# Expert tiles of 128 places at the end of an expert's list, in the expert layer of a conv-attention hybrid

## The chip, the cores and the metric

The kernel runs on one core of a Trainium2 chip, in one launch. The metric is the device time in microseconds; the time of a kernel is the median of its runs.

## What is computed

The reference is four layers over 4 images of 1,024 tokens with 256 channels, all float32: a Mamba-like layer with a squeeze gate, a non-local block, attention followed by a mixture of experts (layer 2), and an efficient attention followed by an LSTM (layer 3). The change lies in the mixture of experts:

```python
B, L, D, H, E = (8, 4096, 256, 1024, 8)         # sizes of H and E are used; D is 256
xf = x.reshape(-1, D)                           # 4096 tokens, normalised
gate_logits = xf @ Wg + bg
top_w, top_i = jax.lax.top_k(gate_logits, 2)
top_w = jax.nn.softmax(top_w, axis=-1)
w_dense = jnp.sum(jax.nn.one_hot(top_i, E) * top_w[..., None], axis=1)
out = 0
for e in range(E):
    h = jax.nn.gelu(xf @ W1[e] + b1[e], approximate=False)
    out = out + w_dense[:, e:e + 1] * (h @ W2[e] + b2[e])
```

Every token picks two of eight experts, so there are 8,192 picks. The input is fixed by a seed, and so is how many picks each expert gets.

## The kernel before

The kernel does not compute all eight experts for all tokens. It sorts the picks into lists, one for each expert, and cuts every list into tiles of `TW` = 256 places, each of `SUB` = 2 groups of 128 places (one place for each partition). The last tile of a list is padded with places that point to spare rows.

**Two lots.** The first lot, `early`, has `EARLY` = 16 tiles made from the first three images, and it is planned while the attention of the fourth image still runs (`_plan_early`, L906). The second lot, `late`, has the rest. Only a number of late tiles that always suffices can be unrolled without a test; `TILES` = 23 is the most that can come about, `FIRM` = 20 are run always, and the three beyond lie behind a branch. The branch tests `v.used`, the number of late tiles that the lists need, which each engine reads into a register (L830, L831).

**The plan.** `_plan_late` (L941) works on VectorE: it takes the number of picks of each expert from a small matmul, counts the tiles in it by comparing with 0, 256, 512 and so on (L947, L948), subtracts those taken early, and sums up to the end and the begin of each expert's tiles. `_tile_weights` (L878) turns this into the row of the expert's weights for every tile. `_of_picks` (L892) looks up one number for each pick, such as where its expert begins. `_table` (L1003) compares the place of each pick with all places (L1016), and 64 small bf16 matmuls into `p_t` (L1024) turn that into the list of rows to gather, `rows`, and a mark for first or second choice, `second`. The table of the late lot is made beside the first early tiles.

**One tile.** `_expert_tiles` (L1119) runs the tiles of a list in order. For each one:

- Weights: one indirect DMA on GpSimd's queue (L1091) gathers the whole expert, 128 rows of 4,360 float32 numbers, into one of three buffers. It is issued two tiles ahead.
- Rows: two indirect DMAs (L1101), one for each group of 128 places, issued three tiles ahead.
- `turn`: four transposes (L1128) into `p_x` and one copy to `xT` on VectorE (L1132), one tile ahead.
- First product: for each of 8 parts of the hidden layer, two matmuls with 256 columns (L1152) into `ph`, which has two buffers, and a Gelu with bias on ScalarE (L1155) into `hT`.
- Second product: for each group of 128 places, eight matmuls with 256 columns (L1162) into `po`, which has two buffers; then bias and gate on VectorE (L1173, L1174) and a scatter-add into `acc` in DRAM (L1175, GpSimd's queue).

When all tiles are done, `acc` is read back into `rows` for layer 3 (L1732).

**Order of the work.** The experts' stage is ordered by a planner that places the instructions of each engine by its own estimate of costs; within an engine the order is then fixed. The layers' LSTM at the end is ordered by hand. A float32 matmul leaves two records in the trace, a transpose one.

Of the kernel before, what the change touches and what calls it, by code (L numbers as in the profile page):

```python
# [9 lines left out]
F32 = mybir.dt.float32  # L10
# [8 lines left out]
P = 128  # L19
# [24 lines left out]
SUB = TW // P  # L44
NE = NT - TPI
EARLY = (2 * NE * P - E * (TW - 1)) // TW
TILES = (2 * T + E * (TW - 1)) // TW - EARLY
FIRM = 2 * T // TW + E // 2 - EARLY
G = 16
AWAY = 1024.0  # L50
NMOE = C * HID + NHC * D + NHC + D
# [751 lines left out]
        s.last.append(lambda: _plan_late(s, single))  # L803


def _layer2_experts(s, beside):

    nc, tc, v = s.nc, s.tc, s.plan
    with ExitStack() as ctx:
        pool = ctx.enter_context(tc.tile_pool(name="moe", bufs=2))
        ps = ctx.enter_context(tc.tile_pool(name="moe_ps", bufs=2, space=PSUM))
        s.fetch.pools.append(pool)

        def aside(k):  # L820
            if k == 0:
                p = ps.tile([P, 2, TILES * SUB], F32, name="p_t", bufs=1)
                _table(s, pool, p, v.late)
            if k == EARLY // 2:
                beside()

        for f in s.last:
            f()
        _expert_tiles(s, pool, ps, s.tiles, aside)
        used = nc.values_load(v.used[0:1, 0:1], min_val=0, max_val=TILES)  # L830
        with tc.If(used > FIRM):  # L831
            tiles = [(v.late, i) for i in range(FIRM, TILES)]
            _fetch_first(s, tiles)
            _expert_tiles(s, pool, ps, tiles)
    s.choice.close()
# [39 lines left out]
        s.nc.vector.tensor_add(v.before[:, n, :], v.before[:, n - 1, :], both[:, n - 1 - first, :])  # L875


def _tile_weights(s, tab):  # L878

    nc, v = s.nc, s.plan  # L880
    n = tab.tiles
    past = v.past[:, :n, :]
    nc.vector.tensor_tensor(past, _bc(tab.end, 1, n), _bc(v.by_tile[:, :n], 2, E), ALU.is_le)
# [3 lines left out]
    nc.vector.scalar_tensor_tensor(  # L887
        tab.weights, expert, float(P), v.slot.to_broadcast([P, n]), ALU.mult, ALU.add
    )


# [14 lines left out]
def _plan_early(s, pool, slim):  # L906


    nc, v = s.nc, s.plan
    tab = v.early  # L910
    count = slim()[:, :E]
    nc.tensor.matmul(count, s.ones, v.before[:, NE, :], start=True, stop=True)

    nc.vector.scalar_tensor_tensor(
        v.over, _bc(count, 2, T // TW), 0.5 - TW, _bc(v.edge, 1, E), ALU.add, ALU.is_gt
    )
    full = v.full
    nc.vector.tensor_reduce(full, v.over, AX.X, ALU.add)
    nc.vector.tensor_tensor_scan(tab.end, s.ones[:, :E], full, 0.0, ALU.mult, ALU.add)
    nc.vector.tensor_sub(tab.begin, tab.end, full)  # L920
    nc.vector.tensor_scalar(v.taken, tab.begin, -1.0, float(EARLY), ALU.mult, ALU.add)
    nc.vector.tensor_scalar_max(v.taken, v.taken, 0.0)
    nc.vector.tensor_tensor(v.taken, v.taken, full, ALU.min)
    _tile_weights(s, tab)
    stop = pool.tile([P, E], F32, name="stop")
    nc.vector.tensor_add(stop, tab.begin, v.taken)
    for x in (tab.begin, stop):
        nc.vector.tensor_scalar_mul(x, x, float(SUB))
    half = v.half[:, :NE].rearrange("p n i -> p (n i)")
    tab.place = _of_picks(s, pool, "which", tab.begin, NE)  # L930
    nc.vector.tensor_add(tab.place, tab.place, half)
    done = _of_picks(s, pool, "stops", stop, NE)
    nc.vector.tensor_tensor(done, tab.place, done, ALU.is_lt)
    nc.vector.scalar_tensor_tensor(half, done, AWAY, half, ALU.mult, ALU.add)
    nc.vector.tensor_scalar(done, done, -AWAY, AWAY, ALU.mult, ALU.add)
    nc.vector.tensor_add(tab.place, tab.place, done)
    p = slim()[:, : 2 * EARLY * SUB].rearrange("p (v h) -> p v h", v=2)
    _table(s, pool, p, tab)


def _plan_late(s, slim):  # L941

    nc, v = s.nc, s.plan
    tab = v.late
    count = slim()[:, :E]
    nc.tensor.matmul(count, s.ones, v.before[:, NT, :], start=True, stop=True)
    nc.vector.tensor_tensor(v.over, _bc(count, 2, T // TW), _bc(v.edge, 1, E), ALU.is_gt)  # L947
    nc.vector.tensor_reduce(v.full, v.over, AX.X, ALU.add)  # L948
    nc.vector.tensor_sub(v.full, v.full, v.taken)
    nc.vector.tensor_tensor_scan(tab.end, s.ones[:, :E], v.full, 0.0, ALU.mult, ALU.add)  # L950
    nc.vector.tensor_sub(tab.begin, tab.end, v.full)
    nc.vector.tensor_sub(tab.begin, tab.begin, v.taken)
    nc.vector.tensor_scalar_mul(tab.begin, tab.begin, float(SUB))
    _tile_weights(s, tab)
    nc.vector.tensor_copy(v.used, tab.end[:, E - 1 :])
    tab.place = None


# [44 lines left out]
def _table(s, pool, p_t, tab):  # L1003
# [1 line left out]


    nc, v = s.nc, s.plan
    n, h = tab.tokens, tab.tiles * SUB
    place = tab.place
    if place is None:  # L1010
        place = _of_picks(s, pool, "place", tab.begin, n)
        nc.vector.tensor_add(place, place, v.half[:, :n].rearrange("p n i -> p (n i)"))
    for g in range(2 * n // G):
        at = bass.ts(g, G)
        own = pool.tile([P, G, h], BF16, name="own")
# [27 lines left out]
def _plan_constants(s, pool):  # L1043
    nc = s.nc
    v = s.plan = SimpleNamespace()
    v.picks = pool.tile([P, NT, 2, E], BF16, name="picks")
    v.half = pool.tile([P, NT, 2], F32, name="half")
    v.left = pool.tile([P, NT, 2, P], BF16, name="left")
    v.before = pool.tile([P, NT + 1, E], F32, name="before")
    n = max(EARLY, TILES)  # L1050
    for name, shape in (
        ("over", [E, T // TW]), ("full", [E]), ("taken", [E]), ("past", [n, E]), ("expert", [n]),
    ):
        setattr(v, name, pool.tile([P, *shape], F32, name=name))
    v.used = pool.tile([P, 1], I32, name="used")
    for name, tokens, tiles in (("early", NE, EARLY), ("late", NT, TILES)):
        tab = SimpleNamespace(tokens=tokens, tiles=tiles, xn=s.xn if tokens == NT else s.xn_early)
        for key, shape, dtype in (
            ("end", [E], F32), ("begin", [E], F32), ("weights", [tiles], I32),
            ("rows", [tiles * SUB], I32), ("second", [tiles * SUB, 2], F32),  # L1060
        ):
# [4 lines left out]
    v.halves = _iota(s, pool, "halves", n * SUB, 1)  # L1066
# [12 lines left out]
def _fetch(s, pool):  # L1079
# [16 lines left out]

    def rows(tab, i):
        got = []
        for j in range(SUB):
            r = pool.tile([P, D + 2], F32, name=f"r{j}", bufs=4)  # L1100
            nc.gpsimd.indirect_dma_start(  # L1101
                out=r, out_offset=None, in_=tab.xn, in_offset=at(tab.rows, i * SUB + j)
            )
            got.append(r)
        f.got.append(got)

    f.weights, f.rows, f.at = weights, rows, at


def _fetch_first(s, tiles):  # L1110
# [8 lines left out]
def _expert_tiles(s, pool, ps, tiles, aside=None):  # L1119
# [2 lines left out]
    nc, tc, f = s.nc, s.tc, s.fetch  # L1122

    def turn(rows):
        p_x = ps.tile([P, C, TW], F32, name="p_x", bufs=1)
        for j in range(SUB):
            for k in range(C):
                nc.tensor.transpose(  # L1128
                    p_x[:, k, bass.ts(j, P)], rows[j][:, bass.ts(k, P)], s.ident
                )  # L1130
        xT = pool.tile([P, C, TW], F32, name="xT")
        nc.vector.tensor_copy(xT, p_x)  # L1132
        return xT

    xT = turn(f.got[0])
    for i, (tab, number) in enumerate(tiles):
# [8 lines left out]
            f.rows(*tiles[i + 3])  # L1145
        if i + 2 < len(tiles):
            f.weights(*tiles[i + 2])
        hT = pool.tile([P, NHC, TW], F32, name="hT")
        for m in range(NHC):
            ph = ps.tile([P, TW], F32, name="ph")  # L1150
            for k in range(C):
                nc.tensor.matmul(  # L1152
                    ph, w1[:, k, bass.ts(m, P)], xT[:, k, :], start=k == 0, stop=k == C - 1
# [1 line left out]
            nc.scalar.activation(hT[:, m, :], ph, AF.Gelu, bias=b1[:, m : m + 1])  # L1155
        if i + 1 < len(tiles):
            xT = turn(f.got[0])
        for j in range(SUB):
            n = number * SUB + j
            po = ps.tile([P, D], F32, name="po")  # L1160
            for m in range(NHC):
                nc.tensor.matmul(  # L1162
# [546 lines left out]
def conv_attn_hybrid_kernel(ctx: ExitStack, tc: tile.TileContext, d: dict, out: bass.AP):  # L1709
# [121 lines left out]
```

## Time and profile before

| | |
|---|---|
| median of 3 runs | 3441.82 us (3440.3 to 3443.47) |
| the profiled execution's own time | 3442.45 us |
| its span, from first to last instruction | 3440.7 us |
| mean granted TensorE clock | 0.985 |
| TensorE busy, share of the span | 3119.8 us, 91% |
| VectorE, ScalarE, GpSimd busy | 1837.7, 1097.0, 533.3 us |
| first and last matmul of L1152 | 710.5 us and 1226.4 us |
| last scatter-add issued, `acc` read back | 1235.8 us, 1241.9 us |

The experts' stage is thus some 525 us of 3,441. In the lines of the profile, L12 is line 12 of the kernel before. A group's row has the line, the engine, the operation, what it writes and reads with shapes, and its number; then the busy time in us and the mean duration of one in ns; then the idle time of the engine before it and what ended most of that. PE is TensorE's matmul, PEld its weight load (shown apart, since it overlaps), DVE is VectorE, ACT ScalarE, POOL GpSimd, SP SyncE. In order of time, a row has the start and the duration in us, and in brackets the idle time ahead and what ended it. A busy TensorE is not TensorE at its peak, because the ends of matmuls are modelled and overlap; the spacing from start to start says what one costs in a row of them.

### The profile page before, as it was taken

The numbers are of one execution on the slowest core, as the hardware profiler recorded it, in microseconds if no ns is written. First come the engines' busy times: TensorE is split into PE (matmuls) and PEld (weight loads), VectorE is DVE, ScalarE is ACT, GpSimd is POOL, SyncE is SP. The second block draws the span as 40 slices with busy tenths as digits, with TensorE's granted clock in tenths as the row PEclk, the third lists the DMA queues.
The fourth block names the chain that finished last, engine by engine and source line by source line (L and its number), as shares of the span: only waits on it lengthen the run. The fifth ranks groups of instructions, "written<-read, shape, count | busy, mean of one in ns | idle before, by whom it ended". The sixth has DMA issues, their size and how long they took to land.

```text
span 3440.7 us, 143780 instructions
## 1 busy us (share of the span) xinstructions
PE 3119.8 (91%) x63650; PEld 2505.1 (73%) x63650; DVE 1837.7 (53%) x8205; ACT 1097.0 (32%) x4339; POOL 533.3 (16%) x749
## 2 busy tenths in 40 slices
PE   8797899999999989998998998998998998998887
PEld 5476577678888856777777777777777777777776
DVE  5785644651111143565555565655655665555555
ACT  5763222222222222332332332332332332332222
POOL 2252100124444320001001001001001001001000
PEclk9898999999999989999999999999999999999999
DMA  2000011356666620000000000000000000000000
GB/s 82 1 1 2 9 37 38 107 168 197 193 193 193 189 62 1 4 4 9 5 4 8 6 4 9 6 4 8 6 4 8 6 4 8 6 4 8 7 4 10
DMA packets 49459, 138.94 MB, mean 40 GB/s; under 512 B 4992, under 2 KB 38336, under 8 KB 44224
## 3 DMA queue, kind: packets, MB, share of 16 engines
q0 software_dynamic: 19008, 99.32, 9.4%
q1 hardware_dynamic: 27680, 24.45, 2.2%
q8 instruction: 499, 8.18, 1.0%
q10 hardware_dynamic: 2144, 5.95, 0.5%
q14 instruction: 128, 1.05, 0.1%
HBM read 104.21 MB, written 25.49 MB: 38 GB/s over the span
## 4 chain that ended last, share of the span: by engine, by line
PE 28%; DVE 20%; ACT 10%; issue 5%; DMA 1%; ACTq 0%; POOL 0%; DVEq 0%; SPq 0%
PE pre L1657 16%; DVE col L1668 11%; PE pre L1600 6%; ACT tri L1671 5%; DVE scan L1680 5%; DVE hs L1691 4%; PE p_a L1554 3%; PE p_d L1258 1%; PE p_k L1226 1%; DMA acc<-y,late_rows 1%; ACTq L1671 0%; PE p_w L165 0%; PE p_d L1266 0%; PE p_w L1246 0%; PE p_u L1388 0%
## 5 line engine op out<-in xcount | busy, mean ns | idle before, releaser
L1657 PE MATMUL pre<-w_v,hs 128*4 128x64 f32 x49104 | 872.9, 219 | 210.2 <-DVE hs L1691 199.2
L1657 PEld LDWEIGHTS pre<-w_v,hs 128*4 128x4 f32 x49104 | 684.1, 86 | 398.8 <-DVE hs L1691 397.1
L1600 PE MATMUL pre<-xg,pick 128*128 128x64 f32 x6144 | 903.9, 283 | 0.5 <-DVE xg L1567 0.5
L1600 PEld LDWEIGHTS pre<-xg,pick 128*128 128x128 f32 x6144 | 763.5, 191 | 118.4 <-DVE xg L1567 1.2
L1668 DVE STREAM_TRANSPOSE col<-pre 128x64 f32<-128x64 f32 x2048 | 485.2, 250 | 304.5 <-PE pre L1657 289.2
L1671 ACT ACTIVATE tri<-col 128x16 f32<-128x16 f32 x1024 | 229.4, 224 | 1178.6 <-DVE col L1668 1178.6
L1680 DVE TENSOR_TENSOR_SCAN scan<-tri 128x24 f32<-128x24 f32 x1024 | 216.3, 211 | 361.8 <-ACT tri L1671 361.8
L1562 POOL TENSOR_TENSOR xg<-xg,gate_bias 128x192 f32<-128x192 f32 x127 | 74.8, 589 | 1605.6 <-ACT xg L1561 1605.6
L1152 PE MATMUL ph<-xT,wt 128*128 128x256 f32 x1152 | 256.3, 380 | 1.6 <-issue 0.9
L1162 PE MATMUL po<-wt,hT 128*128 128x256 f32 x1152 | 255.7, 379 | 0.0
L1155 ACT ACTIVATE hT<-ph,wt 128x256 f32<-128x256 f32 x288 | 136.1, 473 | 360.2 <-PE ph L1152 354.3
L1152 PEld LDWEIGHTS ph<-xT,wt 128*128 128x128 f32 x1152 | 207.1, 189 | 43.2 <-ACT hT L1155 6.1
L1162 PEld LDWEIGHTS po<-wt,hT 128*128 128x128 f32 x1152 | 216.0, 190 | 27.8
L1689 DVE STREAM_TRANSPOSE gate<-row 128x64 f32<-128x64 f32 x1024 | 228.3, 223 | 0.7
L1678 ACT ACTIVATE row<-pre 128x64 f32<-128x64 f32 x1024 | 210.3, 205 | 0.6
L1696 DVE SCALAR_TENSOR_TENSOR tri<-hs,scan 128x8 f32<-128x8 f32 x1023 | 182.1, 178 | 36.2 <-DVE hs L1691 1.7
L1132 DVE COPY xT<-p_x 128x512 f32<-128x512 f32 x36 | 24.9, 691 | 211.2 <-PE p_x L1128 211.0
L1173 DVE TENSOR_TENSOR y<-po,wt 128x256 f32<-128x256 f32 x72 | 30.6, 424 | 193.9 <-PE po L1162 184.3
L1554 PE MATMUL p_a<-w_u,u 128*32 128x192 f32 x1792 | 119.3, 338 | 0.0
L732 PE MATMUL p_s<-u,q 128*128 128x512 f32 x256 | 117.0, 597 | 0.0
L766 PE MATMUL p_w<-v,prT 128*128 128x256 f32 x512 | 116.0, 379 | 0.7 <-ACT prT L758 0.7
L766 PEld LDWEIGHTS p_w<-v,prT 128*128 128x128 f32 x512 | 95.5, 190 | 15.5 <-issue 2.9
(2441 smaller groups left out, 3287.6 us busy)
## 6 DMA issues: line engine op xcount, KB each, us to landing
xn<-xn SPq DMA_DIRECT2D x8, 516.0 KB, 3.6
x<-in_x_dram SPq DMA_DIRECT2D x16, 256.0 KB, 2.9
acc<-rows SPq DMA_DIRECT2D x8, 512.0 KB, 2.9
out_dram<-part SPq DMA_DIRECT2D x64, 64.0 KB, 1.7
xn_early<-xn SPq DMA_DIRECT2D x6, 516.0 KB, 4.9
rows<-acc SPq DMA_DIRECT2D x6, 512.0 KB, 8.1
w_l<-in_w_l_dram ACTq DMA_DIRECT2D x1, 1092.0 KB, 10.2
rows<-acc SPq DMA_DIRECT2D x4, 256.0 KB, 4.2
```

The lines of the kernel that those rows point to most:

```text
L766: nc.tensor.matmul(p, prT[:, n, :], images[g // TPI].v[:, n, :], start=n == 0, stop=n == TPI - 1)
L1152: nc.tensor.matmul(ph, w1[:, k, bass.ts(m, P)], xT[:, k, :], start=k == 0, stop=k == C - 1)
L1162: nc.tensor.matmul(po, hT[:, m, bass.ts(j, P)], w2[:, m, :], start=m == 0, stop=m == NHC - 1)
L1554: nc.tensor.matmul(p[32 * j : 32 * (j + 1), :], u3[i * SG // P][:, k, bass.ts(i % (P // SG), 32)], w_u[:, k, j * Q : (j + 1) * Q], start=k ...
L1600: nc.tensor.matmul(p, pick[:, r].rearrange("p j r -> p (j r)"), xg[i][:, v], start=True, stop=t == 0,)
L1657: nc.tensor.matmul(p[32 * j : 32 * j + B, :], hs[:, t - 1, k * B : (k + 1) * B], w_v[:, k, j * Q + v.start : j * Q + v.stop], start=False, ...
L1668: nc.vector.transpose(col[:, g * C : (g + 1) * C, :].rearrange("p n r -> p (n r)"), pre[t % 2][g])
L1671: nc.scalar.activation(z[:, 2:50].rearrange("p (g q) -> p g q", g=2)[:, :, ::3].rearrange("p g (k b) -> p (g k) b", k=C), col[:, :, :B], A ...
L1678: nc.scalar.activation(row, pre[t % 2][2], AF.Tanh)
L1680: nc.vector.tensor_tensor_scan(scan, z[:, 0 : 3 * S], z[:, 26 : 26 + 3 * S], 0.0, ALU.mult, ALU.add)
L1689: nc.vector.transpose(gate.rearrange("p n r -> p (n r)"), row)
L1696: nc.vector.scalar_tensor_tensor(tri[(t + 1) % 2][:, 28:52:3], h, 0.5, cell, ALU.mult, ALU.mult)
```

## The change

A list may now end in a half tile. If the rest of an expert's picks over full tiles is 1 to 128, that rest goes into a tile of one group of 128 places; a rest of 129 to 255 still makes a full tile. The second lot consists of `TILES` = 19 full tiles and `HALVES` = 8 half tiles at most. Of these 17 full and 4 half tiles are always run; the half ones lie after the 4th, 8th, 12th and 16th full tile of the late lot, and the last tile is a full one. The 2 full and 4 half tiles beyond lie behind the branch, which now tests whether more than 17 full or more than 4 half tiles are needed. A half tile gathers the expert's whole weights and one group of rows, transposes two blocks, runs its first product with 128 columns and its second product for one group. The plan counts full tiles and half tiles apart and gives the picks of an odd end their own places, behind all full ones. The early lot is not changed.

```diff
-TILES = (2 * T + E * (TW - 1)) // TW - EARLY
-FIRM = 2 * T // TW + E // 2 - EARLY
+TILES = (2 * T + E * (P - 1)) // TW - EARLY
+HALVES = E
+FIRM = 2 * T // TW + 1 - EARLY
+FIRM_HALVES = E // 2
...
+def _late(tab, first, last, first_half, last_half):
+
+    tiles = [(tab, i) for i in range(first, last)]
+    n = last_half - first_half
+    step = max(len(tiles) // n, 1)
+    for i in reversed(range(n)):
+        tiles.insert(step * (i + 1), (tab, TILES + first_half + i))
+    return tiles
...
-                p = ps.tile([P, 2, TILES * SUB], F32, name="p_t", bufs=1)
+                p = ps.tile([P, 2, v.late.places], F32, name="p_t", bufs=1)
...
-        used = nc.values_load(v.used[0:1, 0:1], min_val=0, max_val=TILES)
-        with tc.If(used > FIRM):
-            tiles = [(v.late, i) for i in range(FIRM, TILES)]
+        rest = nc.values_load(v.rest[0:1, 0:1], min_val=0, max_val=TILES)
+        with tc.If(rest > 0):
+            tiles = _late(v.late, FIRM, TILES, FIRM_HALVES, HALVES)
...
-    nc.vector.tensor_tensor(v.over, _bc(count, 2, T // TW), _bc(v.edge, 1, E), ALU.is_gt)
-    nc.vector.tensor_reduce(v.full, v.over, AX.X, ALU.add)
+
+    for i in range(2):
+        nc.vector.scalar_tensor_tensor(
+            v.over, _bc(count, 2, T // TW), float(-P * i), _bc(v.edge, 1, E), ALU.add, ALU.is_gt
+        )
+        n = (v.begun, v.full)[i]
+        nc.vector.tensor_reduce(n, v.over, AX.X, ALU.add)
+    odd, v.stop, v.odd_end, v.jump = v.odd, v.begun, v.early.end, v.early.begin
+    nc.vector.tensor_sub(odd, v.begun, v.full)
+
+    nc.vector.tensor_scalar_mul(v.stop, v.full, float(SUB))
...
-    _tile_weights(s, tab)
-    nc.vector.tensor_copy(v.used, tab.end[:, E - 1 :])
+    nc.vector.tensor_tensor_scan(v.odd_end, s.ones[:, :E], odd, 0.0, ALU.mult, ALU.add)
+    nc.vector.tensor_sub(v.jump, v.odd_end, odd)
+    nc.vector.tensor_sub(v.jump, v.jump, v.stop)
+    nc.vector.tensor_sub(v.jump, v.jump, tab.begin)
+    nc.vector.tensor_scalar_add(v.jump, v.jump, float(TILES * SUB))
+    _tile_weights(s, tab.weights[:, :TILES], tab.end)
+    _tile_weights(s, tab.weights[:, TILES:], v.odd_end)
+
+    left = v.over[:, 0, :2]
+    nc.vector.tensor_scalar_add(left[:, 0:1], tab.end[:, E - 1 :], -float(FIRM))
+    nc.vector.tensor_scalar_add(left[:, 1:2], v.odd_end[:, E - 1 :], -float(FIRM_HALVES))
+    nc.vector.tensor_tensor(left[:, 0:1], left[:, 0:1], left[:, 1:2], ALU.max)
+    nc.vector.tensor_scalar_max(left[:, 0:1], left[:, 0:1], 0.0)
+    nc.vector.tensor_copy(v.rest, left[:, 0:1])
...
         place = _of_picks(s, pool, "place", tab.begin, n)
-        nc.vector.tensor_add(place, place, v.half[:, :n].rearrange("p n i -> p (n i)"))
+        nc.vector.tensor_add(place, place, half)
+        stop = _of_picks(s, pool, "stop", v.stop, n)
+        nc.vector.tensor_tensor(stop, half, stop, ALU.is_ge)
+        jump = _of_picks(s, pool, "jump", v.jump, n)
+        nc.vector.tensor_mul(jump, jump, stop)
+        nc.vector.tensor_add(place, place, jump)
...
-        for j in range(SUB):
+        for j, place in enumerate(_places(i)):
             r = pool.tile([P, D + 2], F32, name=f"r{j}", bufs=4)
...
+def _places(i):
+
+    return range(i * SUB, (i + 1) * SUB) if i < TILES else (TILES * SUB + i - TILES,)
...
-        p_x = ps.tile([P, C, TW], F32, name="p_x", bufs=1)
-        for j in range(SUB):
+        n = len(rows) * P
+        p_x = ps.tile([P, C, TW], F32, name="p_x", bufs=1)[:, :, :n]
+        for j in range(len(rows)):
...
-        hT = pool.tile([P, NHC, TW], F32, name="hT")
+        places = _places(number)
+        width = len(places) * P
+        hT = pool.tile([P, NHC, TW], F32, name="hT")[:, :, :width]
         for m in range(NHC):
-            ph = ps.tile([P, TW], F32, name="ph")
+            ph = ps.tile([P, TW], F32, name="ph")[:, :width]
...
-        for j in range(SUB):
-            n = number * SUB + j
+        for j, n in enumerate(places):
...
-        s.tiles = [(v.early, i) for i in range(EARLY)] + [(v.late, i) for i in range(FIRM)]
+        s.tiles = [(v.early, i) for i in range(EARLY)] + _late(v.late, 0, FIRM, 0, FIRM_HALVES)
```

More of the change, by code (lines that the diff above doesn't have):

```diff
@@ L875, in _before, with _tile_weights @@
         s.nc.vector.tensor_add(v.before[:, n, :], v.before[:, n - 1, :], both[:, n - 1 - first, :])
-def _tile_weights(s, tab):
+def _tile_weights(s, weights, end):
     nc, v = s.nc, s.plan
-    n = tab.tiles
+    n = weights.shape[1]
     past = v.past[:, :n, :]
-    nc.vector.tensor_tensor(past, _bc(tab.end, 1, n), _bc(v.by_tile[:, :n], 2, E), ALU.is_le)
+    nc.vector.tensor_tensor(past, _bc(end, 1, n), _bc(v.by_tile[:, :n], 2, E), ALU.is_le)
     expert = v.expert[:, :n]
@@ L887, in _tile_weights @@
     nc.vector.scalar_tensor_tensor(
-        tab.weights, expert, float(P), v.slot.to_broadcast([P, n]), ALU.mult, ALU.add
+        weights, expert, float(P), v.slot.to_broadcast([P, n]), ALU.mult, ALU.add
     )
@@ L923, in _plan_early @@
     nc.vector.tensor_tensor(v.taken, v.taken, full, ALU.min)
-    _tile_weights(s, tab)
+    _tile_weights(s, tab.weights, tab.end)
     stop = pool.tile([P, E], F32, name="stop")
@@ L953, in _plan_late @@
     nc.vector.tensor_scalar_mul(tab.begin, tab.begin, float(SUB))
-    _tile_weights(s, tab)
-    nc.vector.tensor_copy(v.used, tab.end[:, E - 1 :])
+    nc.vector.tensor_tensor_scan(v.odd_end, s.ones[:, :E], odd, 0.0, ALU.mult, ALU.add)
[11 more added lines that the diff above has]
+    nc.vector.tensor_copy(v.rest, left[:, 0:1])
     tab.place = None
@@ L1007, in _table @@
     nc, v = s.nc, s.plan
-    n, h = tab.tokens, tab.tiles * SUB
+    n, h = tab.tokens, tab.places
     place = tab.place
     if place is None:
+        half = v.half[:, :n].rearrange("p n i -> p (n i)")
         place = _of_picks(s, pool, "place", tab.begin, n)
-        nc.vector.tensor_add(place, place, v.half[:, :n].rearrange("p n i -> p (n i)"))
+        nc.vector.tensor_add(place, place, half)
[4 more added lines that the diff above has]
+        nc.vector.tensor_add(place, place, jump)
     for g in range(2 * n // G):
@@ L1052, in _plan_constants @@
         ("over", [E, T // TW]), ("full", [E]), ("taken", [E]), ("past", [n, E]), ("expert", [n]),
+        ("begun", [E]), ("odd", [E]),
     ):
         setattr(v, name, pool.tile([P, *shape], F32, name=name))
-    v.used = pool.tile([P, 1], I32, name="used")
-    for name, tokens, tiles in (("early", NE, EARLY), ("late", NT, TILES)):
-        tab = SimpleNamespace(tokens=tokens, tiles=tiles, xn=s.xn if tokens == NT else s.xn_early)
+    v.rest = pool.tile([P, 1], I32, name="rest")
+    for name, tokens, tiles, halves in (("early", NE, EARLY, 0), ("late", NT, TILES, HALVES)):
+        places = tiles * SUB + halves
+        tab = SimpleNamespace(
+            tokens=tokens, places=places, xn=s.xn if tokens == NT else s.xn_early
+        )
         for key, shape, dtype in (
-            ("end", [E], F32), ("begin", [E], F32), ("weights", [tiles], I32),
-            ("rows", [tiles * SUB], I32), ("second", [tiles * SUB, 2], F32),
+            ("end", [E], F32), ("begin", [E], F32), ("weights", [tiles + halves], I32),
+            ("rows", [places], I32), ("second", [places, 2], F32),
         ):
@@ L1065, in _plan_constants @@
     v.lanes = _iota(s, pool, "lanes", P, 1, base=1)
-    v.halves = _iota(s, pool, "halves", n * SUB, 1)
+    v.halves = _iota(s, pool, "halves", n * SUB + HALVES, 1)
     v.edge = _iota(s, pool, "edge", T // TW, TW)
@@ L1098, in rows @@
         got = []
-        for j in range(SUB):
+        for j, place in enumerate(_places(i)):
             r = pool.tile([P, D + 2], F32, name=f"r{j}", bufs=4)
             nc.gpsimd.indirect_dma_start(
-                out=r, out_offset=None, in_=tab.xn, in_offset=at(tab.rows, i * SUB + j)
+                out=r, out_offset=None, in_=tab.xn, in_offset=at(tab.rows, place)
             )
@@ L1130, in turn @@
                 )
-        xT = pool.tile([P, C, TW], F32, name="xT")
+        xT = pool.tile([P, C, TW], F32, name="xT")[:, :, :n]
         nc.vector.tensor_copy(xT, p_x)
```

## The prediction

> **What bounds the kernel now.** I first read the page: the span, the busy shares in 40 slices and the dear groups. The change touches only the experts' stage of layer 2 and its planning, so the rest of the page (the 1,024-step LSTM from slice 16 on) matters only in that it starts when this stage ends. Then I asked the busy time of the stage.
>
> ```profile
> span 3440.7 us, 143780 instructions
> ...
> L1152 PE MATMUL ph<-xT,wt 128*128 128x256 f32 x1152 | 256.3, 380 | 1.6 <-issue 0.9
> L1162 PE MATMUL po<-wt,hT 128*128 128x256 f32 x1152 | 255.7, 379 | 0.0
> L1155 ACT ACTIVATE hT<-ph,wt 128x256 f32<-128x256 f32 x288 | 136.1, 473 | 360.2 <-PE ph L1152 354.3
> ```
>
> ```profile
> 749.20:907.00 157.80, 157.80 (x751) 135.28 (x750) 26.67 (x98) 41.81 (x89) 67.89 (x56) 1.00 0.64 194
> 907.00:1234.00 327.00, 326.66 (x1555) 279.58 (x1553) 54.80 (x205) 86.90 (x184) 130.28 (x105) 1.00 0.59 178
> ```
>
> Columns of the second fence: the stretch and its length, then busy time of TensorE, its weight loads, VectorE, ScalarE and GpSimd, granted clock, DMA share, GB/s. TensorE has no idle time in 484 us, the clock is full, the DMA engines are 64% busy at most. TensorE alone sets this stage's length. 1,152 records of L1152 are 36 tiles of 32 records (a float32 matmul leaves two): 16 early and 20 late tiles ran, and the branch did not.
>
> One tile in order of time:
>
> ```profile
> 1005.61 7.09 PE L1152 MATMUL ph<-xT,wt 128*128 128x256 f32 x32
> 1006.73 0.47 ACT L1155 ACTIVATE hT<-ph,wt 128x256 f32<-128x256 f32 x1 [7.78 <-PE ph L1152]
> 1007.01 0.94 POOL L1091 DMA_INDIRECT wt<-in_moe_dram,late_weights  x1 [0.68 <-issue]
> 1007.25 5.05 PEld L1152 LDWEIGHTS ph<-xT,wt 128*128 128x128 f32 x24 [0.15 <-ACT hT L1155]
> 1012.54 0.60 PE L1128 MATMUL p_x<-ident,r 128*128 128x128 f32 x4
> 1012.97 7.07 PE L1162 MATMUL po<-wt,hT 128*128 128x256 f32 x32
> 1019.88 7.09 PE L1152 MATMUL ph<-xT,wt 128*128 128x256 f32 x32
> ```
>
> From 1005.61 to 1019.88 a full tile takes 14.27 us. Spacing of records: (7.07 - 0.379) / 31 = 0.2158 us; 64 of these plus 4 transposes at 0.109 ((0.60 - 0.273) / 3) make 14.25.
>
> **Does the branch stay untaken?** Working the reference's router through on its inputs gives 1028, 1110, 951, 1181, 1178, 916, 984 and 844 picks per expert. Rounded up to 256 that is 36 tiles, which the trace confirms. Under the new rule a rest of 1 to 128 makes a half tile: rests are 4, 86, 183, 157, 154, 148, 216, 76, so 33 full and 3 half tiles. 33 - 16 early = 17, exactly the firm number, and 3 is under 4. So 16 + 17 full and 4 half tiles run, one half tile for nothing, and the branch is skipped.
>
> **Removed: three full tiles.** 3 x 14.27 = 42.8 us, all on TensorE's path.
>
> **Added: four half tiles.** The second product keeps its shape (256 columns) and halves its number: 16 records x 0.2158 = 3.45 us. The first keeps its 32 records but streams 128 columns. No such row is in this stage; the nearest is L441, float32, a 128x128 load ahead of each record, 128 columns:
>
> ```profile
> 212.67 1.16 PE L441 MATMUL p_o<-diag,zs 128*128 128x128 f32 x8
> ```
>
> Its 11 in a row at 215.27 take 1.39 us: (1.39 - 0.275) / 10 = 0.1115. So 32 x 0.1117 = 3.57 us. Here a rule of the Trainium skill speaks against the change: TensorE: Matmul & The Clock Gate, Part 3, "The mechanism", says that a weight load overlaps running matmuls only when it goes to other row groups (Part 2 of the page also lets it go to a background buffer), and "LDWEIGHTS (loading the stationary operand)" prices 128 columns at 128 / 1.2 = 107 ns. Load and stream in turn would make 0.107 + 0.11 = 0.22 us per record, 7.0 us for the product, no cheaper than a full tile's. The row decides: at 0.2158 per 256 columns and 0.1117 per 128 columns the load is hidden.
>
> But ScalarE now comes into play. `ph` has two buffers, so group m+2 (four records) waits for the Gelu of group m. In the full tile above, the first group's last record starts at 1006.26; its Gelu at 1006.73 (0.38 for the record, 0.09 of signal, 0.04 in later groups); the next load 0.05 after its end, its matmul some 0.1 later. That just fits 0.86 us per group. For a half tile: Gelu of 128 columns = 473 less what a copy from PSUM loses between 256 and 128 columns:
>
> ```profile
> L1262 ACT COPY ut<-p_d 128x256 f32<-128x256 f32 x8 | 3.0, 372 | 23.9 <-PE p_d L1258 23.9
> L1583 ACT COPY part<-p_a 128x128 f32<-128x128 f32 x64 | 17.0, 265 | 4.3
> ```
>
> 473 - 107 = 366 ns. From the last record's start: 0.275 + 0.04 + 0.366 + 0.05 + 0.1 = 0.83 us to group m+2, against 5 x 0.1117 = 0.56 without the wait. So TensorE stands 0.27 us ahead of groups 2, 4 and 6 (0.32 the first time). In the changed program's order the next tile's four transposes lie one behind each pair of groups, so three fall into these gaps. First product: 3.57 + 0.32 + 0.27 + 0.27 = 4.43, the fourth transpose 0.11, second product 3.45: 8.0 us. The tile ahead does two transposes fewer (0.22): net 7.78 per half tile, 31.1 for four. Bounds: no stall at all, 3.57 + 0.22 + 3.45 = 7.24 (29.0); Gelu not shorter at all (0.473), 8.1 (32.4). The near rows give the middle.
>
> **Fetches.** 37 weight fetches in place of 36, each still a whole expert (2.2 MB), and 70 scatter-adds in place of 72.
>
> ```profile
> 1007.00:1016.60 9.60, 9.60 (x48) 8.13 (x47) 0.77 (x3) 3.51 (x8) 3.53 (x3) 1.00 0.80 271
> 1016.60:1021.30 4.70, 4.70 (x23) 4.13 (x23) 1.63 (x6) 0.30 (x1) 2.58 (x2) 1.00 0.25 32
> ```
>
> A fetch is issued 1.4 us into tile i (1007.01) for tile i+2 and has drained by 1016.6, 9.6 us later. With a half tile among the two, i+2 starts 14.27 + 7.78 = 22 us after i: some 11 us to spare; two fetches that overlap behind a half tile cost 2 of these. GpSimd's queue in a half tile: two gathers (2 x 0.98), one weight fetch (0.94), two scatter-adds left by the tile ahead (2 x 1.6), 6.1 us of 7.78. So nothing is added; without this cover each late fetch would stop TensorE for what it lacks.
>
> **Planning on VectorE.** Some 26 operations are new between L947 and L1016, and the third tile's copy of `xT` (0.69) moves ahead of the table. The table keeps its width (19 x 2 + 8 = 46 places, before 23 x 2). Before:
>
> ```profile
> 736.24 0.42 DVE L898 TENSOR_TENSOR mine<-picks,place_e 128x512 bf16<-128x512 bf16 x1
> 736.69 0.69 DVE L902 TENSOR_REDUCE place<-mine 128x64 f32<-128x512 bf16 x1
> 737.67 1.76 DVE L1016 TENSOR_TENSOR own<-halves,place 128x736 bf16<-128x736 f32 x2
> 740.64 0.83 PE L1024 MATMUL p_t<-right,left 128*128 128x92 bf16 x16 [0.24 <-DVE right L1021]
> ```
>
> Two more sums over the picks (2 x 1.17 from start to start), three finishing operations (0.66), the copy (0.65), a second comparison and reduction (0.5) and some 18 tiny ones at 0.05 to 0.08: about 5 us later. Queued behind: TensorE's 64 table matmuls, in program order, and behind them the third tile. The changed order puts ten more `po` matmuls (20 records, 4.3 us) ahead of the table, so TensorE reaches it at 744.7 and finds it at about 745.4 to 746.2: a wait of 0.7 to 1.5 in place of 0.24 + 0.33. Plus 0.5 us; bounds 0 and 2. The late rows are first gathered three tiles ahead of tile 16, over 100 us later.
>
> **The seam behind.** The last tile is still a full one and the branch is skipped as before: last scatter-add, its landing, the loads of `rows`.
>
> ```profile
> 1235.80 1.54 POOL L1175 DMA_INDIRECT acc<-y,late_rows  x1 [2.93 <-DVEq L831]
> 1241.87 9.33 SPq L1732 DMA_DIRECT2D rows<-acc  x10
> ```
>
> Nothing changes there; all else keeps its order on every engine.
>
> **Sum.** 42.8 - 31.1 - 0.5 = 11.2 us. The profiled execution took 3442.45 (span 3440.7), so 3431.2; the median of the runs is 3441.8, which makes 3430.6.
>
> **Rivals.** (a) The load is not hidden at 128 columns: a half tile costs 7.0 + 3.45 + 0.1 = 10.5, four cost 42, no change, 3441. Against it: L441. (b) Weights come late, each half tile lasts as long as a fetch (9.6): 4 x 1.8 = 7.3 lost, 3438. For it: a half tile is shorter than a fetch. Against it: 11 us of slack, and four full tiles between half ones. (c) The other side: the branch is taken. Then 2 full and 4 half tiles follow, 28.5 + 31.1, after a cold fetch of about 11 us in the open: 71 us more, 3501. It decides as soon as the full tiles pass 33 or the half ones 4. Full tiles stand at the limit, but the nearest half tile (rest 86) lacks 43 picks to become full, and a full one that shrinks (rest 148, 20 picks) makes the fourth half tile, still inside. A different rounding of the logits moves a few picks, not 43.
>
> **How the numbers follow.** Forecast 0.88; (a) 0.03; (b), or a table stall of several us, 0.06; (c) 0.03. The forecast's own bounds: half tiles give 10.4 to 13.8, the table takes 0 to 2, and runs differ by 1.6 either way: gains of about 7 to 15. Range 3426 to 3435.5, which leaves out part of (b) and all of (a) and (c). A measurement tells 0.2% (6.9 us) from no change: faster 0.91, same 0.05, slower 0.04.
>
> **What would show it.** L1152 at 256 columns x1056 and at 128 columns x128, spaced near 0.112 with gaps near 0.16 to 0.27 in which TensorE's loads wait for L1155's successor; Gelu of 128 columns near 366 ns; 132 + 8 transposes; a half tile of 8.0 us from first record to first; no TensorE wait for a weight fetch; the first table matmul near 745. I am wrong if rows of the branch's tiles run, if half tiles take over 8.5 us, or if a wait for weights or rows appears.

## The result

The changed kernel takes 3423.09 us, the median of 5 runs from 3422.7 to 3423.79. The kernel before takes 3440.3 us, the median of 5 runs from 3433.49 to 3443.47, of which two ran beside the changed kernel. The ratio of the two is 0.9947, with a 95% interval from 0.9936 to 0.9958. That is 17.2 us less between the medians, where 11.2 were forecast; 3423.09 lies 2.9 us below the low end of the stated range.

The experts' stage shows what the prediction said it would. These are rows of the costliest groups of the changed kernel, with each shape of tile kept apart:

```profile
L1213 PE MATMUL po<-wt,hT 128*128 128x256 f32 x1120 | 248.9, 379 | 0.0
L1204 PE MATMUL ph<-xT,wt 128*128 128x256 f32 x1056 | 235.6, 380 | 1.6 <-issue 0.9 <-ACT hT L1207 0.7
...
L1204 PE MATMUL ph<-xT,wt 128*128 128x128 f32 x128 | 18.1, 284 | 0.0
...
L1207 ACT ACTIVATE hT<-ph,wt 128x128 f32<-128x128 f32 x32 | 11.8, 368 | 34.1 <-PE ph L1204 31.9 <-issue 1.2
```

L1204, L1207 and L1213 are the first product, the Gelu and the second product, before L1152, L1155 and L1162. 1,056 records are 33 full tiles, 128 are four half tiles, and so the branch was not taken. The Gelu of 128 columns lasts 368 ns (366 forecast).

TensorE in order of time, around the first half tile, with two rows of its weight loads (PEld):

```profile
997.10 7.07 PE L1213 MATMUL po<-wt,hT 128*128 128x256 f32 x32
1003.80 1.08 PEld L1204 LDWEIGHTS ph<-xT,wt 128*128 128x128 f32 x8
1004.01 1.05 PE L1204 MATMUL ph<-xT,wt 128*128 128x128 f32 x8
1004.90 0.27 PE L1178 MATMUL p_x<-ident,r 128*128 128x128 f32 x1
1005.12 0.97 PEld L1204 LDWEIGHTS ph<-xT,wt 128*128 128x128 f32 x8 [0.19 <-ACT hT L1207]
1005.13 1.16 PE L1204 MATMUL ph<-xT,wt 128*128 128x128 f32 x8
1006.12 0.27 PE L1178 MATMUL p_x<-ident,r 128*128 128x128 f32 x1
1006.29 1.16 PE L1204 MATMUL ph<-xT,wt 128*128 128x128 f32 x8
1007.29 0.27 PE L1178 MATMUL p_x<-ident,r 128*128 128x128 f32 x1
1007.46 1.16 PE L1204 MATMUL ph<-xT,wt 128*128 128x128 f32 x8
1008.46 0.27 PE L1178 MATMUL p_x<-ident,r 128*128 128x128 f32 x1
1008.57 3.62 PE L1213 MATMUL po<-wt,hT 128*128 128x256 f32 x16
1012.02 7.09 PE L1204 MATMUL ph<-xT,wt 128*128 128x256 f32 x32
```

From 1004.01 to 1012.02 a half tile takes 8.01 us (8.00 forecast). Two groups of the first product, 8 records, stand together, then one transpose of the next tile fills part of the wait for the Gelu: 1.16 to 1.17 us from pair to pair. Pairs that need not wait would follow each other after 8 x 0.1117 + 0.109 = 1.00 us, so some 0.16 us of wait are left; only ahead of the second pair does the profile name it, as 0.19 us of the loads' wait for the Gelu. Inside the first pair the records stand close: 7 spacings plus the last record's 0.275 make 1.05, so (1.05 - 0.275) / 7 = 0.111 us each. The eight loads of this pair, 1.08 us long, lie beside its matmuls: the weight load is hidden at 128 columns too.

The busy time by stretches of the changed kernel, in the same columns as the second fence of the prediction:

```profile
757.00:907.00 150.00, 150.00 (x716) 128.57 (x715) 26.01 (x96) 38.93 (x82) 66.13 (x54) 1.00 0.64 193
907.00:1214.00 307.00, 307.00 (x1515) 263.93 (x1514) 51.32 (x193) 86.50 (x190) 123.54 (x100) 1.00 0.63 195
```

TensorE still stands nowhere by this measure, and the list of waits between 745 and 1,221 us names no wait of TensorE for weights; the one wait inside is that of its loads for the Gelu, 5.3 us in 34 pieces. The kernel before has 5.2 us in 34 pieces there, so that list does not show what a half tile waits; the spacing of its rows does.

So where do the other 6 us come from? The two profiled executions lie 18.8 us apart in their spans, which divide as follows, from the trace's rows (the end of the stage is the last expert matmul's start plus its spacing of 0.216 us, here and below): 1.1 us ahead of the stage (the first expert matmul starts at 709.43 instead of 710.51), 11.9 inside it (511.05 instead of 522.98), 2.65 between its end and the first step of the LSTM (127.22 instead of 129.87), and 3.1 in the LSTM (2066.83 instead of 2069.91 from the first scan to the last). The change adds no instruction in three of these four parts.

### The profile page after: what moved, and what is told of

It is laid out like the page before. It is cut to its first block, busy times and chain, and to the rows that moved or that the text cites. A ratio compares the mean times of both kernels' runs of the same rounds, so it can differ in the third digit from the quotient of the medians.

```text
span 3422.0 us, 143796 instructions
## 1 busy us (share of the span) xinstructions
PE 3104.9 (91%) x63646; PEld 2493.8 (73%) x63646; DVE 1837.6 (54%) x8224; ACT 1099.1 (32%) x4347; POOL 529.4 (15%) x746
## 4 chain that ended last, share of the span: by engine, by line
PE 54%; DVE 26%; ACT 11%; issue 6%; POOL 2%; DMA 1%; ACTq 0%; DVEq 0%; SPq 0%; POOLq 0%
PE pre L1708 16%; DVE col L1719 11%; PE ph L1204 7%; PE po L1213 7%; PE pre L1651 6%; ACT tri L1722 5%; DVE scan L1731 5%; DVE hs L1742 4%; PE p_a L1605 3%; PE p_w L768 3%; PE p_s L734 3%; DVE acc L299 1%; PE p_o L486 1%; PE p_d L1309 1%; PE p_w L755 1%
## 5 line engine op out<-in xcount | busy, mean ns | idle before, releaser
L1204 PE MATMUL ph<-xT,wt 128*128 128x256 f32 (+1 forms) x1184 | 253.7, 370 | 1.6 <-issue 0.9
L1207 ACT ACTIVATE hT<-ph,wt 128x256 f32<-128x256 f32 (+1 forms) x296 | 136.9, 463 | 353.6 <-PE ph L1204 346.6
L1213 PE MATMUL po<-wt,hT 128*128 128x256 f32 x1120 | 248.9, 379 | 0.0
L1204 PEld LDWEIGHTS ph<-xT,wt 128*128 128x128 f32 x1184 | 205.6, 189 | 41.6 <-ACT hT L1207 6.2
L1213 PEld LDWEIGHTS po<-wt,hT 128*128 128x128 f32 x1120 | 209.9, 190 | 27.0
L1182 DVE COPY xT<-p_x 128x512 f32<-128x512 f32 (+1 forms) x37 | 24.5, 662 | 205.7 <-PE p_x L1178 205.6
```

The costliest lines, as they stand in the source:

```text
L1204: nc.tensor.matmul(ph, w1[:, k, bass.ts(m, P)], xT[:, k, :], start=k == 0, stop=k == C - 1)
L1213: nc.tensor.matmul(po, hT[:, m, bass.ts(j, P)], w2[:, m, :], start=m == 0, stop=m == NHC - 1)
```

## The experiments

Two theories were set against each other. By the first the change is worth what its stage shows, some 12 us, and the rest is the scatter between executions. By the second the change also makes what comes behind it faster, and would do so in every run. Both kernels were timed again in three later sessions, each on another chip, beside kernels with one to three edits; the kernel before was profiled again in the first two of them, the changed kernel in all three.

### Both kernels again

Edit: none. `e1_before` and `e5_before` are the kernel before, `e2_after`, `e6_after` and `e10_after` the changed one, in three sessions.

> The kernel before, once more. From the last expert matmul to the first LSTM scan the first profile took 129.9 us here and 127.2 in the changed kernel; from the first to the last scan 2069.9 against 2066.8; up to the first expert matmul 710.5 against 709.4. Theory A (these 6.9 us are chance of the execution: the windows of the TensorE clock fall differently, and the LSTM's step differs by 2 ns): this profile differs from the first one by as much, in either direction, and ten or more runs of this kernel spread over 5 us or more. Theory B (they come from the change: all that follows the shorter stage gets a better place): this profile repeats 710.5, 129.9 and 2069.9 within 0.5 us. Ratio to before 1.000 in both.

> The changed kernel, once more. Theory A: up to the first expert matmul, between the last one and the first scan, and over the LSTM the three stretches move by up to some us against 709.4, 127.2 and 2066.8, and the median is 11 to 14 us below that of the kernel before on this chip (ratio 0.996 to 0.9967). Theory B: the three stretches repeat within 0.5 us, and the median stays 16 to 19 us below (ratio 0.9945 to 0.9953). In both each half tile takes 8.0 us and the experts' stage from first to last matmul 511 us (before 523).

> The kernel before, a third profile. Theory A (what differs outside the experts' stage is chance of the execution and of the chip): stage 523.0 us, and the stretches ahead of it, behind it to the first LSTM scan, and the LSTM vary about 709, 130 and 2070 by 1 to 3 us. A later look at the LSTM's step (median 2.006 us in the first profile of the changed kernel, 2.008 in all others) should show it to go with the session, not with the kernel: if this profile has 2.006, so has the next one.

> The changed kernel, a third profile and five more rounds. Theory A: 12 to 15 us below the kernel before on this chip; stage 511.1 us; outside of it stretches as in the kernel before within 3 us in sum. Theory B (4 to 6 us come from the change outside the stage): 16 to 19 us below.

> The changed kernel, a fourth profile and five more rounds. If its first times of 3423 us were those of one session (LSTM step of 2.006 us, three cold clock windows in a row behind the stage and no more), this is again 13 to 14.5 us below the kernel before; if the kernel itself has two levels, some rounds fall at 3423 on this chip too. Stage 511.2 us in both.

Timed: e1_before against its own copy 1.0001 [0.9993, 1.0009] and e5_before 1.0001 [0.9994, 1.0008], so two equal kernels compare as equal. Their times were 3436.62 to 3443.28 in 13 runs and 3435.6 to 3447.26 in 18. The changed kernel, each time beside the runs of the kernel before in the same session:

| | before, median | changed, median | gain | ratio, 95% |
|---|---|---|---|---|
| e2_after | 3440.87 (17 runs) | 3426.56 | 14.3 | 0.9961 [0.9947, 0.9975] |
| e6_after | 3442.28 (25 runs) | 3428.84 | 13.4 | 0.9960 [0.9946, 0.9974] |
| e10_after | 3438.20 (9 runs) | 3424.84 | 13.4 | 0.9965 [0.9951, 0.9978] |

The means give gains of 13.6, 13.7 and 12.8 us in place of 14.3, 13.4 and 13.4, and the interval of each ratio is some 9 us wide (8.6 to 18.2 for e2_after). The 17.2 us do not come back; the first theory had 11 to 14, 12 to 15 and 13 to 14.5, which the medians meet within 0.3.

The profiled executions, cut at four rows that each trace has: the first matmul of the experts and the end of the last, the first and the last scan of the LSTM, which has one scan in each of its 1,024 steps (us).

| | to the stage | stage | stage to LSTM | LSTM | span |
|---|---|---|---|---|---|
| before | 710.51 | 522.98 | 129.87 | 2069.91 | 3440.74 |
| e1_before | 707.01 | 523.06 | 130.28 | 2070.70 | 3438.51 |
| e5_before | 704.46 | 522.70 | 129.99 | 2069.28 | 3433.88 |
| after | 709.43 | 511.05 | 127.22 | 2066.83 | 3421.96 |
| e2_after | 708.38 | 511.19 | 129.05 | 2068.79 | 3424.84 |
| e6_after | 709.69 | 511.26 | 130.04 | 2070.36 | 3428.79 |
| e10_after | 704.92 | 511.16 | 130.34 | 2067.70 | 3421.56 |
| mean of before | 707.33 | 522.91 | 130.05 | 2069.96 | |
| mean of changed | 708.11 | 511.17 | 129.16 | 2068.42 | |

The stage gains 11.7 us, and each trace gives it within 0.3. Everything else makes 1.7 us less in the mean (+0.8, -0.9, -1.5), while one and the same kernel moves there by 6.6 us (before) and 7.1 us (changed), span less stage. Three and four traces can't tell 1.7 from nothing. The 2.65 us between stage and LSTM and the 3.1 in the LSTM do not come back in every trace: e6_after has 130.04 and 2070.36 there, like the kernel before.

One small part looks as if it came back: from the last expert matmul to the first matmul on the rows read back, the kernel before takes 11.86, 11.87 and 11.90 us, the changed one 11.11, 11.28, 11.41 and 11.76, 0.5 less in the mean. The end of that wait, for the kernel before (the prediction shows its beginning):

```profile
1245.36 3.75 PE L1277 MATMUL p_w<-rows,ident 128*128 128x256 f32 x8 [11.70 <-DMA rows<-acc]
```

and the wait for the changed one:

```profile
1222.67 1.54 POOL L1226 DMA_INDIRECT acc<-y,late_rows  x1 [2.81 <-DVEq L843]
...
1228.42 9.02 SPq L1783 DMA_DIRECT2D rows<-acc  x10
...
1231.60 3.75 PE L1328 MATMUL p_w<-rows,ident 128*128 128x256 f32 x8 [10.95 <-DMA rows<-acc]
```

The last expert matmul lies at 1233.49 and 1220.48, so the read is issued 8.38 and 7.94 us behind it. But two of the kernels below, e3_three and e7_best, which end their lot with the same full tile as the changed one, take 12.12 and 11.82 us. So these 0.5 us are not shown to belong to the change.

The clock shows what the first trace of the changed kernel had besides. Busy time by stretches, the clock being the third column from the end: the kernel before, the changed one, and the changed one again (e6_after), each from about 5 us behind that first matmul on the rows:

```profile
1250.00:1290.00 40.00, 36.24 (x140) 23.22 (x141) 29.40 (x94) 11.31 (x19) 9.00 (x15) 0.91 0.19 62
```

```profile
1237.00:1277.00 40.00, 36.37 (x146) 22.20 (x147) 29.01 (x94) 11.32 (x19) 8.89 (x14) 1.00 0.17 54
```

```profile
1237.00:1277.00 40.00, 35.95 (x137) 22.29 (x138) 28.77 (x93) 10.77 (x19) 7.99 (x15) 0.91 0.19 62
```

The clock is either full or half in these traces, so 0.91 over 40 us is 7 us at half speed. It changes in windows of 3.413 us; about two of these were at half speed here in the kernel before and in e6_after, and none in the first trace of the changed kernel. Where the windows lie against the program differs from execution to execution, in both kernels.

The traces of all experiments show what goes with this. From the first matmul on the rows read back to the first scan, three executions had only two windows at half speed: the first trace of the changed kernel, e3_three and e8_branch, with 116.1, 116.2 and 116.5 us. The other ten, of both kernels and the edited ones, had 3.7 to 4.6 windows and took 117.8 to 118.6; the kernel before 118.0 to 118.4, the changed one in its later traces 117.8, 118.6 and 118.6. Of the 2.65 us, 0.75 are thus the wait for the rows and 1.9 this stretch. The second theory falls for these: the changed kernel runs through the stretch with either clock, and its gain there goes with the clock. For the 3.1 us of the LSTM, where the clock does not differ, e6_after speaks against it, and their cause stays open (see the last section).

### Three half tiles

```diff
-FIRM_HALVES = E // 2
+FIRM_HALVES = 3
```

The inputs have three half tiles, so the one that runs for nothing is left out. The other three now lie after the 5th, 10th and 15th full tile of the lot.

> Three half tiles firm in place of four; the one left out is empty on these inputs, so the branch stays untaken. Price of a half tile from the trace of the changed kernel: 8.01 us, less 0.22 for two transposes that the tile ahead is spared. Both theories: the experts' stage 7.8 us shorter than with four, 503 us. Theory A: the time falls by 7.8 with 2 or 3 us of play either way. Theory B (the end of the stage matters for what follows): the stretches behind the stage differ from those with four half tiles, as the stage ends at another point of the clock's windows.

Timed 3420.48, 20.4 us under the kernel before (0.9938 [0.9924, 0.9951]). The stage goes from 511.19 to 503.41: 7.78 us, the net price of a half tile in the prediction. Against e2_after of the same session the medians give 6.1, with ranges that are 5 to 7 us wide.

### A third buffer for the first product

```diff
-            ph = ps.tile([P, TW], F32, name="ph")[:, :width]
+            ph = ps.tile([P, TW], F32, name="ph", bufs=3)[:, :width]
```

If the wait for the Gelu is what a half tile has over its records, a third buffer takes it away.

> The changed kernel with three buffers for ph in place of two, so that a half tile's third group of matmuls need not wait for the first Gelu. If the wait of 0.27 us ahead of groups 2, 4 and 6 is what lifts a half tile from 7.5 to 8.0 us, half tiles take 7.4 to 7.5 us, and the stage is 2.2 us shorter (509). If the half tile is limited by something else (weight loads, ScalarE's own pace), it stays at 8.0. Full tiles stay at 14.27.

TensorE in order of time, the same tiles as above:

```profile
1001.64 3.73 PE L1204 MATMUL ph<-xT,wt 128*128 128x128 f32 x32
1005.21 0.60 PE L1178 MATMUL p_x<-ident,r 128*128 128x128 f32 x4
1005.65 3.62 PE L1213 MATMUL po<-wt,hT 128*128 128x256 f32 x16
1009.11 7.07 PE L1204 MATMUL ph<-xT,wt 128*128 128x256 f32 x32
```

The 32 records stand in one row, (3.73 - 0.275) / 31 = 0.1115 us apart (0.1117 forecast; they last 275 ns each in this trace), and the half tile takes 9.11 - 1.64 = 7.47 us: 0.54 less than with two buffers. No load waits for the Gelu here any more. So that wait is what a half tile had over its records: 8.01 less the 7.47 of records and transposes alone. Timed 3423.45 (0.9951 [0.9937, 0.9964]), 3.1 us under e2_after; the stage falls by 4.98 to 506.21. That is more than the 2.2 of four half tiles. Each full tile is 0.02 shorter, and the first three tiles take 50.10 us instead of 52.34. There the planner put the work in another order than with two buffers: three waits of TensorE in e2_after, 0.67 us for the Gelu, 0.79 for `xT` and 0.50 for the table, do not stand in this trace. So 2.2 of the 5.0 us belong to that new order as much as to the buffer. It adds to the edit above: both together

> Three firm half tiles and three buffers for ph. From the traces of the two edits alone: 523.0 to 511.2 with the change, 7.8 less for the empty half tile, 5.0 less for the third buffer (of which 0.55 was of that half tile): stage 498.9 us, 24 us below the kernel before, 3416 to 3417 where that takes 3440.5. If the two share a cost, the stage is 500 or more.

timed 3418.47 (0.9927 [0.9913, 0.994]), with a stage of 498.96. That is 12.3 us less stage than e6_after's 511.26; the medians differ by 10.4, with ranges of 4.6 and 5.7 us.

### The branch taken

```diff
-FIRM_HALVES = E // 2
+FIRM_HALVES = 2
```

Two firm half tiles are too few for these inputs, so that the branch runs: two full and six half tiles.

> Two firm half tiles in place of four: one half tile of these inputs is now not covered, so the branch is taken and runs the 2 full and 6 half tiles beyond. By the prediction's third rival: 2 x 14.27 + 6 x 7.8 = 75.3, a cold fetch of about 11 us in the open, less 2 x 7.8 that are no longer firm: 71 us over the changed kernel, about 3497. If the cold start costs nothing, 60; if code loading behind the branch or late weights cost more, over 80.

One run, 3503.02 us, is 74 us over e6_after (71 forecast for rival c). TensorE in order of time at the seam of firm tiles and branch, with GpSimd's first gathers of rows and of weights for the branch:

```profile
1198.83 7.07 PE L1213 MATMUL po<-wt,hT 128*128 128x256 f32 x32
1209.97 1.02 POOL L1145 DMA_INDIRECT r<-xn,late_rows  x1 [0.30 <-issue]
...
1212.57 0.95 POOL L1135 DMA_INDIRECT wt<-in_moe_dram,late_weights  x1 [0.30 <-issue]
1212.93 0.66 PE L1178 MATMUL p_x<-ident,r 128*128 128x128 f32 x2 [7.03 <-DMA r<-xn,late_rows]
1214.05 0.69 PE L1178 MATMUL p_x<-ident,r 128*128 128x128 f32 x2 [0.46 <-DMA r<-xn,late_rows]
1221.55 2.05 PE L1204 MATMUL ph<-xT,wt 128*128 128x256 f32 x4 [6.81 <-DMA wt<-in_moe_dram,late_weights]
```

The last firm product ends near 1205.7 and the first one behind the branch starts at 1221.55: 15.8 us in which TensorE does four transposes, first waiting for the rows and then for the weights. The prediction had put 11 there. The gather of the rows is issued at 1209.97, after the last scatter-add of the firm tiles (1208.12), and the weights only at 1212.57, one behind the other on GpSimd's queue. The stage is 75.8 us longer than e6_after's; that the whole comes nearer to 71 is chance, since the stretch from the stage to the LSTM was 4.6 us shorter in this execution (125.4).

### The half tiles one behind another at the end

```diff
-    n = last_half - first_half
-    step = max(len(tiles) // n, 1)
-    for i in reversed(range(n)):
-        tiles.insert(step * (i + 1), (tab, TILES + first_half + i))
-    return tiles
+    return tiles + [(tab, TILES + i) for i in range(first_half, last_half)]
```

This is rival b at its hardest: four tiles of 8 us, each with a whole expert's weights to fetch.

> The four half tiles stand in a row at the end of the late lot in place of one behind every four full tiles. Rival (b) of the prediction (weights come late): a fetch takes 9.6 us and a half tile lasts 7.6 to 8.0, so if there were no slack each of the four would lose 1.6 to 2 us and the stage would be some 6 us longer, with TensorE waits for weights. By the slack of 11 us that the prediction worked out, a row of four uses up to 8 of it and TensorE never waits: stage 510.5 us (gaps ahead of groups 4 and 6 filled otherwise). Behind the stage: the last tile now has one scatter-add, which need not wait for another one just ahead, so the read of acc starts about 1 us earlier (11.3 to about 10.3 us from the last matmul to the first one behind).

The second and third of the four, TensorE in order of time (L1200 and L1209 are the two products in this kernel):

```profile
1197.85 1.05 PE L1200 MATMUL ph<-xT,wt 128*128 128x128 f32 x8
...
1205.48 1.05 PE L1200 MATMUL ph<-xT,wt 128*128 128x128 f32 x8
...
1213.11 2.27 PE L1200 MATMUL ph<-xT,wt 128*128 128x128 f32 x16
```

7.63 us each, less than the spread-out 8.01, because some of the second product now fills the wait for the Gelu. No wait for weights appears, so rival b falls even without full tiles between. The stage takes 510.48 us. Timed 3425.15 (0.9960 [0.9945, 0.9976]), the same as e10_after. The rows were read back after 11.54 us, where the expectation had 10.3. The last scatter-add was issued 1.29 us behind the last matmul, in e10_after 2.34, but from that issue to GpSimd's next work, which waits for the landing, 6.6 us passed in place of 5.5.

### All three edits

Three firm half tiles, the third buffer, and the half tiles at the end.

> Three firm half tiles at the end of the lot, and three buffers for ph. From the parts: stage 498.9 us of the version with both edits, with half tiles in a row within 1 us of that, and the read of acc about 1 us earlier by the single scatter-add of the last tile: 24 to 26 us below the kernel before.

Timed 3411.47, 26.7 us under the kernel before and 13.4 under the changed one of the same session; ratio 0.9927 [0.9913, 0.994]. The stage takes 498.94 us, as in e7_best, and the rows are there after 10.67 us (11.82 in e7_best): here the single scatter-add gives the 1 us that it did not give in e9_end. This kernel is faster than the kernel before and the changed one, and so are e3_three and e7_best against the changed kernel of their sessions. The ratio to the kernel before is e7_best's, so the place of the half tiles was not shown to matter to the time. With three firm half tiles in place of four, other inputs take the branch sooner; the one price measured for it is the 74 us above.

## Why the prediction was right in its mechanism and wrong in its size

**What bounds the kernel, and whether the branch stays untaken: right.** TensorE shows no idle time behind the first three tiles of the stage, and 33 full tiles and the four firm half ones ran.

**Removed and added tiles: right.** The half tile takes 8.01 us where 8.00 was the sum; the load is hidden (rival a falls); the Gelu takes 368 ns where 366 was worked out from the two copies; e3_three gives 7.78 us for one half tile where 7.78 stood. Here "TensorE: Matmul & The Clock Gate" of the Trainium skill, Part 3, "The mechanism", does not hold for these records: loads over the same rows lay beside the running matmuls at 0.111 us per record.

**Planning on VectorE: mis-sized by 0.6 us.** The table's inputs came 4.6 us later in e2_after (about 5 forecast) and TensorE reached the table when the step said; the wait was

```profile
743.09 0.83 PE L1064 MATMUL p_t<-right,left 128*128 128x92 bf16 x16 [0.50 <-DVE right L1061]
```

once (0.36 to 0.55 in the four traces), and the second group waited no more. The three first tiles, which hold all of it, took 52.51, 52.59 and 52.25 us before and 52.19, 52.34, 52.38 and 52.31 after: 0.1 less in the mean, where the prediction had 0.5 more. The stage's sum is then 42.8 - 4 x (8.01 - 0.22) + 0.1 = 11.7, and 11.7 is the mean of the traces.

**"Nothing changes there" on the seam: open by 0.5 us.** The read of `acc` waits for the landing of the last scatter-add. The rows came 0.5 us sooner in the mean of the changed kernel's traces, and no sooner in e3_three and e7_best.

**"Runs differ by 1.6 either way": the term that failed.** It came from three runs, and so did the 3441.8 from which the range was counted. The kernel before spans 8.2 us over 17 runs of one session (3436.58 to 3444.82) and 11.7 over the 18 runs of e5_before, and the session's median moves from 3438.2 to 3442.3. Of the 17.2 us of the first comparison, 12.8 to 14.3 come back when it is repeated, which the forecast's own gains of 7 to 15 contain. The rest is luck: a set of runs at the good end of this scatter. The first pair of profiles shows where it lay. The changed kernel's had one window at half speed fewer ahead of the stage (20, not 21; 1.1 us), about two and a half fewer behind it (1.9 us), and an LSTM that was 3.1 us shorter. The two runs of the kernel before that ran beside the changed one, 3440.23 and 3433.49, have a mean of 3436.9, and against this the gain is 13.7; but they are 6.7 us apart. So of the 6.0 us between forecast and result 0.5 are the stage and some 3 to 4.4 are scatter. The remaining 1 to 2.6 us, by which the repeated gains exceed the stage's 11.7, stay open: the intervals are some 9 us wide, and the parts outside the stage move by 7 us in one kernel. The range should have been built from that scatter: 11.2 with several us either way.

**The rivals.** (a), whose 0.22 us per record was an estimate, and (b) are refuted by the records at 128 columns and by e9_end. (c) did not happen. Its price came out within 3 us, 74 measured, but the cold start of 11 us in it measured 15.8.

## What to carry to other kernels

A new tile size can be priced closely from rows of the same kernel: the spacing of its records, plus the wait for the next engine when a buffer comes free late. Half the rows cost 56% of a full tile here (8.01 of 14.27 us), and 52% with a third buffer (7.47). Where a change moves 0.3% of a long kernel, the width of the forecast comes from how far equal executions differ, which three runs do not show: cut several traces of one kernel at the same rows and look at the stages that the change doesn't touch.

## What the runs showed of the hardware that was not expected

The windows of the granted clock, 3.413 us long, do not start with the program (the Trainium skill, "TensorE: Matmul & The Clock Gate", Part 1, "What's actually happening", says so too, and that a kernel's cold matmuls vary by it; the prediction had not made a term of it). Against the first instruction their offset was another one in each of the thirteen profiled executions, between 0.17 and 2.87 us, and 16 to 22 of them were at half speed ahead of the experts' stage. The time to the first expert matmul goes with that number: 704.46 and 704.92 us with 16 (e5_before and e10_after, so with either kernel), 708.38 to 709.69 with 20, 709.98 and 712.66 with 22 (e9_end and e7_best), or about 1.1 us for each window, an estimate from a line through the thirteen.

The median step of the LSTM was 2.006 us in the first session with the changed kernel and in all three kernels of the last session, and 2.007 to 2.009 in all others, with either kernel; over 1,024 steps a difference of 2 ns makes 2 us. The traces with 2.006 are all of changed kernels, but e2_after and e6_after, the same kernel on other chips, have 2.008. In the last session the kernel before, which was not profiled there, also has its lowest median, 3438.2. That fits a difference of session or chip; what sets the step was not found.
